# A deformable convolution and eight expert convolutions: groups of x and of the first layer's result kept in SBUF, the last stage in chunks of eight rows, the table's zeros on another queue

## The chip, the cores and the metric

The kernel runs on one core of one Trainium2 chip, in float32. The metric is device time in microseconds, as the median of several runs. Beside those runs there is one profiled execution, which takes longer; all durations of single instructions are from it.

## What is computed

x has shape (2, 256, 128, 128). Two layers follow each other, each with a residual. `_gn` is a group normalisation over groups of eight channels.

```python
def _L0_conv_ref(x, w_conv, b_conv, w_off, b_off, w_mask, b_mask):
    offset = _conv2d(x, w_off, b_off)                   # 3x3, 18 channels
    mask = sigmoid(_conv2d(x, w_mask, b_mask))          # 3x3, 9 channels
    py, px = base_y + dy, base_x + dx                   # 9 sampling points a pixel
    sampled = _deform_sample(x, py, px) * mask          # bilinear, four corners
    return einsum('bckhw,ock->bohw', sampled, w_conv) + b_conv
x = x + _L0_conv_ref(_gn(x), ...)
# eight experts: 256 -> 8 channels by 1x3, 8 -> 256 channels by 3x1, weighted by probs
x = x + _L1_conv_ref(_gn(x), ...)
```

## The kernel before, in words

Rows of an image are handled in groups of eight (GR) and chunks of four (CR). An image has 16 groups; a group of x, 128 partitions by 2 by 1024 numbers, is 1 MB.

**Table.** Bilinear samples are fetched from a table in DRAM, one for each image. A cell of it holds the 256 normalised channels of a pixel and of the pixel below it (`CELL`, 2 KB), so two neighbouring cells, 4 KB, hold all four corners. Around the image lies a frame of zeros, written by six DMAs a table (lines 130 to 138).

**Head** (lines 396 to 468). Image 0 is loaded (16 tiles `xa`), its statistics are taken (line 411), x is normalised in place (`head_norm`, line 431), transposed by TensorE (`hpt`, line 186), copied from PSUM by ScalarE and VectorE in turn (lines 455 and 457) into `hpx`, which has two buffers, and stored to table 0 (line 194). From the third group on, four of the pieces that compute the first group's offsets (`offsets_of`) are put between groups.

**Stream** (lines 735 to 794). One unit is a row of 128 pixels with one of nine taps; there are 2304. A unit takes one gather by GpSimd's queue (line 513, 128 rows of 4 KB, 15 buffers), one product on ScalarE (line 523), three multiply-adds on VectorE (line 529), two transposes (line 539), for each second unit a copy from PSUM (line 547), and one matmul of 128x512 (line 554), which the profile counts as two instructions, as every float32 matmul. Each engine runs its instructions in the order in which this loop emits them: unit s + 15 is gathered, s + 3 multiplied, s added up, s - 8 matmul-ed. Further work is put into slots of the same loop by `put(slot, piece)`: the loads of x (line 492), offsets of a later group (`offsets_of`, lines 279 to 392), the residual (line 563), statistics (line 567) and the store of a finished group to x1 in DRAM (line 570).

Beside image 0's units, `table_beside` (line 573) builds image 1's table: it loads the image twice, once for statistics and once to normalise, transpose and store, each in steps of eight rows. Beside image 1's units, `experts` (line 632) does the second layer for image 0.

**Experts.** A chunk of four rows is loaded from x1 (`xc`, line 640), normalised (line 645), taken through the 1x3 weights into `ph` (line 662), scaled (line 669), taken through the 3x1 weights into two tiles `pe` for even and odd rows (`back`, line 676, and `back_beside`, line 691, for the neighbouring rows), added to xc (line 705) and stored (line 710).

**Tail** (lines 797 to 807). When all units are done, the last statistics are closed and the experts of image 1 run alone, in the order of rows, loads six chunks ahead.

SP's queue carries all plain DMAs but the zeros and issues them in program order: a DMA that waits holds up those behind it.

Of the kernel before, what the change touches and what calls it, by code (L numbers as in the profile page):

```python
# [28 lines left out]
F32 = mybir.dt.float32  # L29
I32 = mybir.dt.int32  # L30
# [35 lines left out]
LM = 8  # L66


@with_exitstack
def layers(ctx, tc, x, w_om, b_om, w_cv, b_cv, w_in, w_out, probs, out):  # L70
    nc = tc.nc

    def view(t, b):
# [31 lines left out]
    base_i = cp.tile([P, GR, NO], I32, name="base_i")  # L105
    nc.gpsimd.memset(base_i, 0)
    nc.gpsimd.iota(
        base_i[:, :, 0:K2].rearrange("p r (i j) -> p r i j", i=3),
        pattern=[[1, GR], [1, 3], [0, 3]], base=-1, channel_multiplier=0,
    )  # L110
    nc.gpsimd.iota(
        base_i[:, :, K2 : 2 * K2].rearrange("p r (i j) -> p r i j", i=3),
        pattern=[[0, GR], [0, 3], [1, 3]], base=-1, channel_multiplier=1,
    )
    base = cp.tile([P, GR, NO], F32, name="base")
    nc.vector.tensor_copy(base, base_i)
    plain = cp.tile([P, GR, NO], F32, name="plain")
# [10 lines left out]


    for t in tables:  # L130
        side = t[WP - 1 : WP - 1 + (HP - 1) * WP].rearrange("(r c) e -> r c e", c=WP)[:, 0:3]
        z3 = zero.unsqueeze(1).broadcast_to([P, 3, CELL])
        nc.scalar.dma_start(t[0:P], zero)
        nc.scalar.dma_start(t[P : WP - 1], zero[0 : WP - 1 - P])
        nc.scalar.dma_start(t[(HP - 1) * WP + 2 : (HP - 1) * WP + 2 + W], zero)
        nc.scalar.dma_start(side[0:P], z3)
        nc.scalar.dma_start(side[P : HP - 1], z3[0 : HP - 1 - P])
        nc.scalar.dma_start(t[HP * WP - 1 : HP * WP + 2], zero[0:3])
# [51 lines left out]
    def store_cells(b, j, px, r, n):  # L190
# [3 lines left out]
        nc.sync.dma_start(cells(b, GR * j - 1 + r, n), pairs)  # L194

    def store_last(b, px):

        nc.sync.dma_start(cells(b, H - 1, 1)[:, 0, 0:C], px[:, GR])
# [3 lines left out]
    def offset_pieces(norm, oc, psum, tag, name):  # L202
# [3 lines left out]
        spread = oc.tile([P, NH, P], F32, name=f"spread_{name}")  # L206
        nb = oc.tile([P, NU], F32, name=f"nb_{name}")
        by_row = oc.tile([P, 3, NO], F32, name=f"by_row_{name}")
# [58 lines left out]

    stream = ExitStack()
    ctx.enter_context(stream)
    up = pool(stream, "u", 1)  # L270
    ip = pool(stream, "idx", 2)
    p_m = pool(stream, "p_m", 3, space=PSUM)
# [6 lines left out]
    def offsets_of(b, g, given=None):  # L279
# [40 lines left out]
        def t(name, shape, dt=F32):  # L320
            held[name] = ip.tile(shape, dt, tag=name, name=f"{name}_{nm}")
# [74 lines left out]
    with ExitStack() as s:  # L396
        hx = s.enter_context(tc.tile_pool(name="hx", bufs=NG))
# [7 lines left out]
        for g in range(NG):  # L405
            xt = hx.tile([P, NH, GN], F32, tag="hx", name=f"xa_{g}")
# [443 lines left out]
```

## Time and profile before

| | |
|---|---|
| median of 3 runs | 3816.98 us (3816.57 to 3818.22) |
| profiled execution | 4171.85 us, span 4169.7 us, mean TensorE clock 0.944 |
| busy | PE 3546.7 us, DVE 3397.1, ACT 1850.5, POOL 2336.0 |
| moved by DMA | 1469.56 MB, 352 GB/s over the span |
| of this, gathers | 1208.11 MB; plain DMAs of SP 255.41 MB; zeros 2.67 MB |
| last statistic of the head ends | 54.6 us |
| first gather issued | 155.8 us |
| last tap of the stream done | 3969.5 us |

PE is TensorE, PEld its weight loads, DVE VectorE, ACT ScalarE, POOL GpSimd, SP the engine that issues DMAs. A group line of the profile names the source line, the engine, the output and inputs, the shapes, the count, busy time and the mean of one. Busy time is no proof of a bound: what matters is what the last wait in a stage is for.

### The profile page before, as it was taken

Reading aid. Unit: us, or ns where it says so; the run is one execution under the profiler, and the core shown is the slowest. Engines: PE = TensorE matmul, PEld = TensorE weight load, DVE = VectorE, ACT = ScalarE, POOL = GpSimd, SP = SyncE. Lnnn points to the kernel's source line nnn. Section 1 sums busy time; section 2 is a strip of 40 time slices with the busy share of each in tenths; the row PEclk is TensorE's granted clock in tenths of the full one; section 3 lists DMA queues with packets and bytes.
Section 4 is the critical chain, followed back from the end, with each engine's and each line's share of the span. In section 5 each row is a group of like instructions: output and inputs, shape, how many; then the busy total and the mean of one; then the engine's idle time right before and its main releaser. Section 6 shows DMA issues by size and latency. Waiting matters only on the chain. (4 is left out here: it accounts for less than half of the span.)

```text
span 4169.7 us, 52967 instructions
## 1 busy us (share of the span) xinstructions
PE 3546.7 (85%) x14684; PEld 1894.1 (45%) x14684; DVE 3397.1 (81%) x7906; ACT 1850.5 (44%) x3899; POOL 2336.0 (56%) x2337
## 2 busy tenths in 40 slices
PE   3588888888878888888888989988988999988999
PEld 2443334444434444443444444444444444444466
DVE  6499998888878888888888888888888888888822
ACT  2244444545445444444444444444444444444432
POOL 0366655666656656666666665665656566655400
PEclk9699999999999999999999999999999999999999
DMA  9999999999999999999899999999999999989754
GB/s 366 391 367 378 389 361 342 377 380 394 354 384 374 404 357 402 386 383 353 326 351 371 350 352 349 359 364 332 357 351 362 347 367 359 364 325 336 293 187 152
DMA packets 434024, 1469.56 MB, mean 352 GB/s; under 512 B 42030, under 2 KB 43182, under 8 KB 433604
## 3 DMA queue, kind: packets, MB, share of 16 engines
q0 software_dynamic: 331776, 1208.11, 76.7%
q1 hardware_dynamic: 100544, 255.41, 16.3%
q8 instruction: 119, 1.95, 0.2%
q10 hardware_dynamic: 1412, 2.67, 0.2%
q14 instruction: 173, 1.42, 0.1%
HBM read 1328.61 MB, written 137.41 MB: 352 GB/s over the span
## 5 line engine op out<-in xcount | busy, mean ns | idle before, releaser
L529 DVE SCALAR_TENSOR_TENSOR acc<-g,wt,acc 128x256 f32<-128x256 f32 x6912 | 3005.3, 481 | 437.6 <-ACT acc L523 289.9
L513 POOL DMA_INDIRECT g<-table,cidx x2304 | 2324.6, 1009 | 1476.1 <-DVE acc L529 489.5
L554 PE MATMUL po<-sm,wcv 128*128 128x512 f32 x4608 | 2481.3, 621 | 300.6 <-DVE x L563 118.0
L547 ACT COPY sm<-ptr 128x512 f32<-128x512 f32 x1152 | 672.5, 584 | 1840.1 <-PE ptr L539 1126.8
L539 PEld LDWEIGHTS ptr<-idp,acc 128*128 128x128 f32 x4608 | 604.3, 145 | 1652.2 <-issue 1017.7
L523 ACT ACTIVATE acc<-g,wt 128x256 f32<-128x256 f32 x2304 | 1064.1, 506 | 104.7 <-DMA g<-table,cidx 75.4
L539 PE MATMUL ptr<-idp,acc 128*128 128x128 f32 x4608 | 939.0, 286 | 177.4 <-ACT sm L547 63.7
L554 PEld LDWEIGHTS po<-sm,wcv 128*128 128x128 f32 x4608 | 747.9, 197 | 368.4 <-ACT sm L547 149.5
L300 PE MATMUL pu<-wus,x 128*128 128x81 f32 (+2 forms) x1600 | 296.7, 313 | 11.6 <-DMA x<-in_x_dram 9.8
L300 PEld LDWEIGHTS pu<-wus,x 128*128 128x128 f32 x1600 | 238.9, 199 | 14.4 <-DMA x<-in_x_dram 10.3
L705 DVE TENSOR_TENSOR xo<-pe,xc 128x512 f32<-128x512 f32 x128 | 85.0, 686 | 187.5 <-PE pe L691 157.2
L662 PE MATMUL ph<-xcn,win 128*64 128x254 f32 (+1 forms) x1536 | 192.9, 399 | 12.1 <-issue 8.1
L662 PEld LDWEIGHTS ph<-xcn,win 128*64 128x64 f32 x1536 | 109.9, 143 | 74.5 <-issue 22.7
L563 DVE SCALAR_TENSOR_TENSOR x<-po,bcv,x 128x512 f32<-128x512 f32 x128 | 95.5, 746 | 54.3 <-remote 27.9
L676 PE MATMUL pe<-h,wout 128*128 128x256 f32 x512 | 132.0, 390 | 0.3 <-issue 0.3
L669 ACT ACTIVATE h<-ph,pr 128x256 f32<-128x256 f32 x64 | 30.5, 476 | 181.2 <-PE ph L662 134.6
L645 ACT ACTIVATE xcn<-xc,shift,rstd 128x512 f32<-128x512 f32 x128 | 100.0, 806 | 1.4 <-DMA xc<-x 1.4
L676 PEld LDWEIGHTS pe<-h,wout 128*128 128x128 f32 x512 | 91.0, 192 | 20.8 <-issue 12.2
L567 DVE BATCH_NORM_STATS2 stats<-x 128x6 f32<-128x512 f32 x128 | 87.6, 684 | 0.1
L691 PE MATMUL pe<-h,wout 64*128 64x128 f32 x1008 | 74.7, 285 | 0.8 <-issue 0.8
L691 PEld LDWEIGHTS pe<-h,wout 64*128 64x128 f32 x1008 | 62.4, 187 | 16.6 <-issue 16.2
L315 PE MATMUL om<-u,idp 128*128 128x216 f32 x192 | 53.8, 362 | 17.6 <-ACT u L309 16.4
(85 smaller groups left out, 638.6 us busy)
## 6 DMA issues: line engine op xcount, KB each, us to landing
g<-table,cidx POOLq DMA_INDIRECT x2304
x<-in_x_dram SPq DMA_DIRECT2D x32, 1024.0 KB
x<-x SPq DMA_DIRECT2D x32, 1024.0 KB
table<-tpx SPq DMA_DIRECT2D x16, 2048.0 KB
xc<-x SPq DMA_DIRECT2D x64, 512.0 KB
out_dram<-xo SPq DMA_DIRECT2D x64, 512.0 KB
table<-hpx SPq DMA_DIRECT2D x15, 2048.0 KB
xa<-in_x_dram SPq DMA_DIRECT2D x16, 1024.0 KB
```

Source lines behind the costliest of these rows:

```text
L300: nc.tensor.matmul(held["ps", j][:, lo:hi], lhsT=xt[:, h, r * W : (r + 1) * W], rhs=w[:, lo - i + 2 : hi - i + 2], start=(i == 2 and h == ...
L513: nc.gpsimd.indirect_dma_start(out=gt[:], out_offset=None, in_=tables[b][:, :], in_offset=bass.IndirectOffsetOnAxis(ap=idx[:, rr, k : k + ...
L523: nc.scalar.activation(acc, gts[u][:, 0:C], AF.Copy, scale=wt[:, 0, rr, k : k + 1])
L529: nc.vector.scalar_tensor_tensor(accs[u], gt[:, q * C : (q + 1) * C], wt[:, q, rr, k : k + 1], accs[u], ALU.mult, ALU.add)
L539: nc.tensor.transpose(pts[u // 2][:, h, (r % 2) * W : (r % 2 + 1) * W], acc[:, h * P : (h + 1) * P], ident)
L547: nc.scalar.copy(sms[u // CR][:, :, (r - 1) * W : (r + 1) * W], pts.pop(u // 2))
L554: nc.tensor.matmul(pos_[b, ci, m], lhsT=wcv[:, h, k, m * P : (m + 1) * P], rhs=sms[u // CR][:, h], start=(k == 0 and h == 0), stop=(k == K ...
L563: nc.vector.scalar_tensor_tensor(v, pos_.pop((b, ci, m)), bcv[:, m : m + 1], v, ALU.add, ALU.add)
L645: nc.scalar.activation(ns[ci][:, h], xs[ci][:, h], AF.Identity, bias=shift[:, h : h + 1], scale=rstd[:, h : h + 1],)
L662: nc.tensor.matmul(o[:, :, to], lhsT=win[:, h, tap], rhs=rows[:, t, :, of], start=(n == 0), stop=(n == 5),)
L676: nc.tensor.matmul(ps[t][:, m], lhsT=wout[:, 2 * t, m * P : (m + 1) * P], rhs=hs[ci], start=(m == 0), stop=False,)
L691: nc.tensor.matmul(ps[t][:, m, j * W : (j + 1) * W], lhsT=wout[half, 1 + 2 * t, m * P : (m + 1) * P], rhs=hs[c][half, i * W : (i + 1) * W] ...
```

## The change

- **x stays.** Two pools outside the stream hold groups of x: `x` and `x_stay`, three buffers each. The head loads groups 0 to 5 of image 0 straight into them and normalises them into two further buffers (`hn`) in place of the tile itself; the stream doesn't load them again. Because there are only two of these, the first group's offset pieces now come between the row pairs of groups 0 and 1, and the third group is normalised after them.
- **The result stays.** The last three groups of image 0 and the last six of image 1 aren't stored to x1. The experts take them from SBUF, and go through the chunks from the last to the first.
- **Experts in place.** The sum is written over xc, and stored from there; the pool of `xo` is gone. Image 0 has four xc buffers and one normalised one (three and two before).
- **Tail by eight rows.** Image 1's experts take chunks of eight rows: matmuls of up to 512 columns, `pe` of two banks each, additions and stores by half of the channels, normalising put earlier.
- **Zeros.** The twelve DMAs of the tables' frames go from ScalarE's queue at the start to SP's queue, behind x and the weights.
- **Room.** `table_beside` works in steps of four rows (64 loads of 512 KB and 32 stores of 1 MB for 32 loads of 1 MB and 16 stores of 2 MB); temporaries of the offsets have one buffer except the cell numbers and weights; some constants live shorter.

The diff, cut to its core:

```diff
@@ -64,6 +64,7 @@
...
 LM = 8
+XB, XR = 3, 3
@@ -126,16 +127,17 @@
...
-    for t in tables:
+    def frame(b):
+        t = tables[b]
...
-        nc.scalar.dma_start(t[0:P], zero)
...
-        nc.scalar.dma_start(side[0:P], z3)
...
+        nc.sync.dma_start(t[0:P], zero)
...
+        nc.sync.dma_start(side[0:P], z3)
@@ -265,10 +267,24 @@
...
+    xp = pool(ctx, "x", XB, side="right")
+    xr = pool(ctx, "x_stay", XR, side="right")
+    def x_tile(b, g):
+        if g >= NG - XR or b == 0 and XB <= g < XB + XR:
+            return xr.tile([P, NH, GN], F32, tag="xr", name=f"x_{b}_{g}")
+        return xp.tile([P, NH, GN], F32, tag="xt", name=f"x_{b}_{g}")
+    def stays(b, g):
+        return g >= NG - XR - (XB if b == B - 1 else 0)
...
+    iq = pool(stream, "idx_1", 1)
@@ -318,7 +334,9 @@
...
-            held[name] = ip.tile(shape, dt, tag=name, name=f"{name}_{nm}")
+            held[name] = (ip if name in ("cidx", "wt") else iq).tile(
+                shape, dt, tag=name, name=f"{name}_{nm}"
+            )
@@ -394,7 +412,8 @@
...
-        hx = s.enter_context(tc.tile_pool(name="hx", bufs=NG))
+        hx = s.enter_context(tc.tile_pool(name="hx", bufs=NG - XB - XR))
+        hn = s.enter_context(tc.tile_pool(name="hn", bufs=2))
         hp = s.enter_context(tc.tile_pool(name="hpx", bufs=2))
@@ -403,7 +422,10 @@
...
-            xt = hx.tile([P, NH, GN], F32, tag="hx", name=f"xa_{g}")
+            if g < XB + XR:
+                xt = xts[0, g] = x_tile(0, g)
+            else:
+                xt = hx.tile([P, NH, GN], F32, tag="hx", name=f"xa_{g}")
             nc.sync.dma_start(xt, xv[:, :, g * GN : (g + 1) * GN])
             xs.append(xt)
@@ -423,19 +445,25 @@
...
+        for b in range(B):
+            frame(b)
...
         def head_norm(g):
+            v = xs[g]
+            if g < XB + XR:
+                xs[g] = hn.tile([P, NH, GN], F32, tag="hn", name=f"xn_{g}")
             nc.scalar.activation(
-                xs[g][:, 0], xs[g][:, 0], AF.Identity, bias=shift[:, 0:1], scale=rstd[:, 0:1]
+                xs[g][:, 0], v[:, 0], AF.Identity, bias=shift[:, 0:1], scale=rstd[:, 0:1]
             )
             nc.vector.tensor_scalar(
-                xs[g][:, 1], xs[g][:, 1], mean[:, 1:2], rstd[:, 1:2], ALU.subtract, ALU.mult
-            )
+                xs[g][:, 1], v[:, 1], mean[:, 1:2], rstd[:, 1:2], ALU.subtract, ALU.mult
+            )
@@ -446,7 +474,7 @@
...
-            if g + 1 < NG:
+            if g != 1 and g + 1 < NG:
                 head_norm(g + 1)
@@ -456,19 +484,20 @@
...
                 if g == 0:
-                    store_cells(0, g, px, i, 2)
+                    store_cells(0, -1, px, i, 2)
+                for piece in samples[: 2 if g < 2 else 1]:
+                    piece()
+                del samples[: 2 if g < 2 else 1]
+            if g == 1:
+                head_norm(2)
             if g > 0:
-                store_cells(0, g, px, 0, GR)
-            if g > 1:
-                for piece in samples[:4]:
-                    piece()
-                del samples[:4]
+                store_cells(0, GR * g - 1, px, 0, GR)
             last = px
-        store_last(0, last)
+        store_last(0, last[:, GR])
@@ -488,9 +517,9 @@
...
     def load_x(b, g):
-        xt = xp.tile([P, NH, GN], F32, tag="xt", name=f"x_{b}_{g}")
-        nc.sync.dma_start(xt, view(x, b)[:, :, g * GN : (g + 1) * GN])
-        xts[b, g] = xt
+        if (b, g) not in xts:
+            xts[b, g] = x_tile(b, g)
+            nc.sync.dma_start(xts[b, g], view(x, b)[:, :, g * GN : (g + 1) * GN])
@@ -571,22 +600,22 @@
...
-        xq = pool(sides, "tx", 2)
+        xq = pool(sides, "tx", 3)
         pq = pool(sides, "tpx", 2)
...
-            held[what, j] = xq.tile([P, NH, GN], F32, tag="tx", name=f"{what}_{b}_{j}")
-            nc.sync.dma_start(held[what, j], xv[:, :, j * GN : (j + 1) * GN])
-        def of_stats(j, i, h):
-            nc.vector.bn_stats(stats[:, h, j * CPG + i], held["xs", j][:, h, i * N : (i + 1) * N])
+            held[what, j] = xq.tile([P, NH, N], F32, tag="tx", name=f"{what}_{b}_{j}")
+            nc.sync.dma_start(held[what, j], xv[:, :, j * N : (j + 1) * N])
+        def of_stats(j, h):
+            nc.vector.bn_stats(stats[:, h, j], held["xs", j][:, h])
@@ -601,11 +630,11 @@
...
-        for j in range(NG):
+        for j in range(NCH):
             put(slot, lambda j=j: load(j, "xs"))
-            for n, (i, h) in enumerate((i, h) for i in range(CPG) for h in range(NH)):
-                put(slot + 16 + 4 * n, lambda j=j, i=i, h=h: of_stats(j, i, h))
-            slot += 16
+            for h in range(NH):
+                put(slot + 14 + 4 * h, lambda j=j, h=h: of_stats(j, h))
+            slot += 8
...
-        for j in range(NG):
+        for j in range(NCH):
             put(slot, lambda j=j: load(j, "xt"))
...
-            for n, i in enumerate(range(0, GR, 2)):
+            for n, i in enumerate(range(0, CR, 2)):
                 put(slot + 26 + 4 * n, lambda j=j, i=i: turn_rows(j, i))
                 put(slot + 28 + 4 * n, lambda j=j, i=i: keep_rows(j, i))
-            put(slot + 42, lambda j=j: store_cells(b, j, held["px", j], 0, GR))
-            slot += 44
-        put(slot, lambda: store_last(b, held["px", NG - 1]))
-        return slot + 1
-    def experts(b, norm, pools, psum, tag, put_, first, step, ahead):
-        cxp, cnp, chp, cop = pools
+            put(slot + 33, lambda j=j: store_cells(b, CR * j - 1, held["px", j], 0, CR))
+            slot += 22
+        put(slot + 14, lambda: store_last(b, held["px", NCH - 1][:, CR]))
...
+    def experts(b, norm, pools, psums, put_, rows, order, first, step, ahead, early=0):
+        cxp, cnp, chp = pools
+        (php, phtag), (pep, petag) = psums
...
+        n, nj = rows * W, rows // 2
+        count = H // rows
+        banks = NH * n // 2 > 512
         def load(ci):
-            xs[ci] = cxp.tile([P, NH, N], F32, tag="cx", name=f"xc_{b}_{ci}")
-            nc.sync.dma_start(xs[ci], x1v[b][:, :, ci * N : (ci + 1) * N])
+            g, r = divmod(ci * rows, GR)
+            if (b, g) in xts:
+                xs[ci] = xts[b, g][:, :, r * W : r * W + n]
+                return
+            xs[ci] = cxp.tile([P, NH, n], F32, tag="cx", name=f"xc_{b}_{ci}")
+            nc.sync.dma_start(xs[ci], x1v[b][:, :, ci * n : (ci + 1) * n])
@@ -649,87 +686,88 @@
...
-            for n, (h, tap) in enumerate(((0, 1), (1, 1), (0, 0), (1, 0), (0, 2), (1, 2))):
+            ps["h"] = php.tile([P, 512], F32, tag=phtag, name=f"ph_{b}_{ci}")
...
         def back(ci, m):
             for t in range(2):
                 if m == 0:
-                    ps[t] = psum.tile([P, NH, N // 2], F32, tag=tag, name=f"pe_{b}_{ci}_{t}")
...
-                    start=(m == 0), stop=False,
+                    start=(banks or m == 0), stop=False,
...
+            own, edge = slice(0, (nj - 1) * W), slice((nj - 1) * W, nj * W)
+            low, rest = slice(0, W), slice(W, nj * W)
+            parts = [(0, ci, rest, own), (1, ci, own, rest), (0, ci - 1, low, edge), (1, ci + 1, edge, low)]
+            parts = [part for part in parts if 0 <= part[1] < count]
...
+                for i, (t, c, to, of) in enumerate(parts):
+                    half = slice(ER, P) if t == 0 else slice(0, ER)
+                    nc.tensor.matmul(
+                        ps[t][:, m, to], lhsT=wout[half, 1 + 2 * t, m * P : (m + 1) * P],
+                        rhs=hs[c][half, of], start=False,
+                        stop=(banks or m == NH - 1) and all(part[0] != t for part in parts[i + 1 :]),
+                    )
+        def total(ci, t, m):
+            ms = slice(0, NH) if m is None else slice(m, m + 1)
+            v = xs[ci][:, ms].rearrange("p h (j t x) -> p t h j x", t=2, x=W)[:, t]
             nc.vector.tensor_tensor(
-                rows(ps["xo"]), ps[t].rearrange("p h (j x) -> p h j x", x=W), rows(xs[ci]), ALU.add
-            )
-        def store(ci):
...
-            del xs[ci]
...
-            e = first + step * ci
...
+        def store(ci, m):
+            ms = slice(0, NH) if m is None else slice(m, m + 1)
+            nc.sync.dma_start(ov[:, ms, ci * n : (ci + 1) * n], xs[ci][:, ms])
+            if m in (None, NH - 1):
+                del xs[ci]
...
-                    put_(e + 2 * h, lambda ci=ci, h=h: normalise(ci, h))
+                    put_(e - early + 2 * h, lambda ci=ci, h=h: normalise(ci, h))
...
+                at_ = e + 20
+                for m in range(NH) if banks else (None,):
+                    for t in range(2):
+                        put_(at_, lambda c=c, t=t, m=m: total(c, t, m))
+                        at_ += 2 if m is None else 0
+                    put_(at_ - (m is None), lambda c=c, m=m: store(c, m))
+                    at_ += 1
@@ -755,8 +793,9 @@
...
-        pools = expert_pools(sides, 3, 2, 4, 2)
-        experts(0, norms1[0], pools, p_m, "m", put, slot + 36, 33, 33)
+        pools = expert_pools(sides, 4, 1, 4)
+        psums = ((p_m, "m"), (p_m, "m"))
+        experts(0, norms1[0], pools, psums, put, CR, range(NCH - 1, -1, -1), slot + 36, 33, 33)
@@ -783,7 +822,7 @@
...
-                if m == NH - 1 and ci % CPG == CPG - 1:
+                if m == NH - 1 and ci % CPG == CPG - 1 and not stays(b, ci // CPG):
                     put(s + 4, lambda b=b, g=ci // CPG: store_x1(b, g))
@@ -798,10 +837,13 @@
...
-    p_m = pool(ctx, "p_e", 8, space=PSUM)
-    pools = expert_pools(ctx, 8, 3, 4, 4)
+    psums = (pool(ctx, "p_h", 2, space=PSUM), "h"), (pool(ctx, "p_e", 3, space=PSUM), "e")
+    pools = expert_pools(ctx, 10, 3, 4)
     tail = defaultdict(list)
-    experts(1, norms1[1], pools, p_m, "e", lambda slot, piece: tail[slot].append(piece), 0, 24, 24 * 6)
+    experts(
+        B - 1, norms1[B - 1], pools, psums, lambda slot, piece: tail[slot].append(piece), GR,
+        range(NG - 1, -1, -1), 0, 24, 24 * 6, 17,
+    )
```

## The prediction

> **What bounds the kernel now.** I read the page's busy row and its 40 slices first, then the busy time by stage, then the DMA rows of three stretches, then the timeline where the stream ends.
>
> Busy time by stage (start and end in us; busy us of PE, PEld, DVE, ACT, POOL with instruction counts; PE clock, DMA share, GB/s). The rows are: head, first gathers, image 0, image 1, tail.
>
> ```profile
> 0.00:155.00 155.00, 60.23 (x336) 55.13 (x336) 82.68 (x149) 39.45 (x54) 11.35 (x33) 0.87 0.99 368
> 155.00:220.00 65.00, 41.58 (x137) 24.82 (x138) 37.94 (x87) 21.92 (x47) 40.47 (x42) 0.74 0.99 388
> 220.00:2060.00 1840.00, 1553.77 (x5670) 784.14 (x5669) 1599.33 (x3774) 863.91 (x1831) 1135.91 (x1125) 0.94 0.97 375
> 2060.00:3935.00 1875.00, 1670.62 (x6896) 884.10 (x6895) 1604.07 (x3761) 851.53 (x1847) 1141.74 (x1132) 0.96 0.94 351
> ...
> 3964.00:4170.00 206.00, 192.21 (x1545) 132.83 (x1543) 47.64 (x78) 60.56 (x98) 0.00 (x0) 0.98 0.53 172
> ```
>
> The head is DMA (0.99). The stream of 2304 gathers has DMA at 0.94 to 0.97 and VectorE at 86 to 87%, with no other engine nearer. The tail has DMA at 0.53 and TensorE at 93%. So bytes count before 3964 us, and matmul time after it.
>
> DMA rows of 5 to 50 us (x loads, 4 KB packets), then of 80 to 140 us (table stores, 2 KB packets):
>
> ```profile
> DMA packets 5485, 18.37 MB, mean 408 GB/s; under 512 B 350, under 2 KB 350, under 8 KB 5484
> DMA packets 11272, 22.75 MB, mean 379 GB/s; under 512 B 176, under 2 KB 176, under 8 KB 11269
> ```
>
> Both stretches are saturated, so 408 is what 4 KB packets get and 379 what 2 KB packets get. Between 170 and 200 us, gathers alone got 409.
>
> VectorE's longest wait in the list of waits (us in total, times, longest):
>
> ```profile
> DVE acc L529 <- ACT acc L523: 289.9, 78, 10.9
> ```
>
> The timeline at the end of the stream and in the tail (start us, us, instruction, count, idle before):
>
> ```profile
> 3963.20 6.28 PE L554 MATMUL po<-sm,wcv 128*128 128x512 f32 x14
> 3976.66 1.52 ACT L645 ACTIVATE xcn<-xc,shift,rstd 128x512 f32<-128x512 f32 x2 [1.44 <-DMA xc<-x]
> 3989.32 2.80 PE L662 MATMUL ph<-xcn,win 128*64 128x256 f32 x24
> 3992.05 1.99 PE L676 MATMUL pe<-h,wout 128*128 128x256 f32 x8
> 3993.98 1.16 PE L691 MATMUL pe<-h,wout 64*128 64x128 f32 x16
> 3995.07 2.80 PE L662 MATMUL ph<-xcn,win 128*64 128x256 f32 x24
> ```
>
> ACT's product waits for its gather in turn. The last lines give the tail's beat: 3995.07 - 3989.32 = 5.75 us for four rows, TensorE without a gap.
>
> **Which time the sum is made against.** The profiled execution took 4171.85 us (span 4169.7), the median is 3816.98. Its steps are priced in the trace, then carried over. If head (155.8 us to the first gather) and tail (206) last as long untraced, the untraced stream has 3817 - 155.8 - 206 - 2 = 3453 us. It moves 1469.6 MB less 57 (head) less 35 (tail) = 1377 MB, so 399 GB/s, and VectorE's 3267 us of stream work fill 94.6% of it. Here the Trainium skill stands against the row. "Perfetto Trace Analysis", section Roofline, gives some 435 GB/s as the practical ceiling for one core alone; this trace never holds more than about 410. By the row the untraced stream runs at 97% of its DMA and each byte removed is time; by the rule at 92%, below VectorE's share, and little is. I take 0.7 of a byte's price for the stream, 1 and 0 as the ends.
>
> **Part by part.**
>
> *Bytes removed.* A group of x is 1.049 MB. Six x loads of image 0 go (6.3 MB), as do three x1 stores and three x1 loads of image 0 (6.3) and six x1 stores of image 1 (6.3), all in the stream; six x1 loads go in the tail (6.3), where DMA has room. The first three of the x loads lie where the stream starts, at DMA 0.99 with VectorE at 58%: 3.1 MB / 0.408 = 7.7 us, whole. The other 15.7 MB: 38.5 us of DMA time.
>
> *Image 1's table in steps of four rows.* Its 32 loads of 1 MB become 64 of 512 KB, with 2 KB packets: 33.5 MB at 379 in place of 408 is 88.4 - 82.1 = +6.3 us of DMA. Its 16 stores of 2 MB become 32 of 1 MB, packets as before. The skill's "DMA: Bandwidth & Descriptors", section Bandwidth, says to batch to 1 MiB or more, and its Anatomy section puts some 2 us of fixed cost on each DMA: by that, 48 more transfers would cost 96 us. The row says they needn't: the saturated table stores above hold 379 GB/s as several transfers overlap, and the gathers fill the gaps. I take +6.3; the ends are 0 (smaller bursts ahead of gathers could even return a few us) and the 96 of the rival below. ScalarE's normalise becomes 64 x 0.806 (L645, same width) for 32 x 1.236: +12 us on an engine 46% busy. VectorE gets 16 more row copies of 0.298: +4.8, hidden by its idle 13% in the trace; uncovered it would be 4.8 whole.
>
> So the stream beyond its start: 38.5 - 6.3 = 32 us of DMA time, x 0.7 = 22.5.
>
> *Head.* Zeros move from ACT's queue (2.67 MB beside x) to SP's queue behind x and weights. The x loads should then end near 2.5 + 16.8/0.408 = 44 us in place of 52, the last statistic near 47 for 54.5, the first table row 8 us sooner. But the bytes ahead of the table are the same, so only idle DMA can be won: from 50 to 70 us it ran at 0.94 and 0.68, 3.8 us idle. Against it: on SP the 12 zero requests stand before the table stores, with the other requests behind them; and the offset matmuls of the first group (48 at 0.175 = 8.4 us) move from spread over groups 2 to 9 into groups 0 and 1, and group 2's normalise (1.25 us) waits for them, since the unnormalised x stays and only two normalised copies exist. With TensorE at 2.6 us a group plus these, group 1's store comes some 1.3 us after group 0's has drained (5.4 us each). 3.8 - 1.3: -2.5. Ends: -6 (no lag) and +2 (lag doubled, a bubble at group 2).
>
> *Tail.* Per eight rows TensorE needs 2 x 5.75 = 11.5 now: 24 L662 at 0.114, 8 L676 at 0.240 and 16 L691 at 0.068 per four rows. L554's fourteen 512-wide ones run at 0.43 each, so 256 columns cost 0.215, and the fixed part is 0.006 (L662, two halves at once), 0.025 (L676), 0.014 (L691). With the width doubled: 24 x 0.221 = 5.31; 8 x 0.455 = 3.64; L691 becomes 8 of 384 columns at 0.175 and 8 of 128 at 0.068, 1.94. Together 10.9. The run from 3977.5 to 4164.7 is 187.2 us; 16 x 10.9 + 1.4 (start, where ScalarE's wider second half is late) = 175.8: -11.4. The start no longer waits for xc (1.05 us), but its first normalise is 0.44 longer: -0.6. At the end four additions of 0.645 follow the last matmul instead of two: +1.3; the 512 KB store is as long as before. Sum -11, ends -14 (L676 at 0.43 flat, 3.44) and -5 (widths scale with no gain).
>
> *At nothing:* one normalised buffer instead of two for image 0's experts (the next normalise comes 27 slots, over 40 us, after its reader; without that cover ScalarE would wait some 3 us a chunk); single offset temporaries (reused a group later, over 100 us); additions in place; reversed chunks. The four-deep xc buffer is stored 43 slots before it is loaded again, so SP shouldn't block at it.
>
> **Sum.** In the trace at full price: -2.5 - 7.7 - 32 - 11 = -53, a span near 4117. Untraced: -2.5 - 7.7 - 22.5 - 11 = -44, so 3773.
>
> **Rivals.**
> *The whole DMA price.* For it: DMA 0.94 to 0.97, 97% of the best rate seen. Against: in image 1 only 351 GB/s. -53: 3764, to 3745 if the smaller bursts spare gathers some of their 5 to 10 us delays. Chance 0.28.
> *VectorE is the bound untraced.* For it: 94.6%, and 59 additions in 25.81 us at the drained end of the stream, which is 1.31 us a gather. Against: its 290 us of waits for products. Then 22.5 goes and 4.8 is added: -2.5 - 7.7 - 11 + 4.8 = -16, 3801. Chance 0.24.
> *Slower: the halved transfers choke SP's queue.* SP issues in order; a load or a table store that waits for its buffer holds up x, x1 and table rows behind it, and gathers wait for their offsets. For it: SP's queue already waited 283.5 us in 9 times for VectorE's first table row (image 0). Against: per row of image there is as much buffer as before. At 2 us for each of 48 transfers: +96 - 44 = +52, 3869. It decides from 0.9 us each (44 / 48). Chance 0.05.
> My forecast has 0.39, and 0.04 is left for no measurable change.
>
> Faster by over 0.2% (7.6 us, about what measurement can tell from none): 0.39 + 0.28 + 0.24 = 0.91; same 0.04; slower 0.05. The range runs from the first rival's low end, 3745, to just past the VectorE case, 3803.
>
> **What would show it.** Moved bytes near 1444 MB; last statistic near 47 us and first gather near 152; DMA of the stream still over 0.93; tail from the last gathered tap to the end near 195 us in place of 206, beat 10.9 us for eight rows. Wrong: VectorE's share of the stream above 90% in the trace with a span cut under 30 us (then it binds), new SP waits for the table tile, or a head that ends later.

## The result, and the profile after

| | before | after |
|---|---|---|
| median | 3816.82 us (3816.46 to 3818.22, 6 runs) | 3802.51 us (3800.80 to 3803.56, 6 runs) |
| ratio, 95% interval | | 0.9962 [0.9949, 0.9974] |
| profiled execution | 3818.56 us, span 3816.4 (the second) | 3802.63 us, span 3800.9 |

The change saves 14.3 us where 44 were forecast. One thing must be said first, as the numbers can't be understood without it: the profile that the prediction was made from, 4171.85 us, is of a slower execution, not of one that profiling had lengthened. The kernel before, profiled once more, took 3818.56 us, 1 us over the median of the runs beside it. A profiled execution doesn't have to take longer than a run, as the section on the metric says it does. From here on "before" is that second profile, unless the first is named.

Busy time by stage, columns as ahead of the prediction (start and end in us; busy us of PE, PEld, DVE, ACT, POOL; clock, DMA share, GB/s). The kernel before, in its second profile; the rows are head, first gathers, image 0, image 1, tail:

```profile
0.00:155.00 155.00, 58.49 (x336) 53.29 (x336) 82.60 (x149) 39.42 (x54) 11.30 (x33) 0.87 0.99 368
155.00:220.00 65.00, 48.36 (x176) 28.44 (x177) 48.59 (x112) 27.66 (x56) 46.18 (x46) 0.77 1.03 409
220.00:1954.00 1734.00, 1527.03 (x5728) 772.45 (x5729) 1618.57 (x3811) 910.08 (x1854) 1160.96 (x1139) 0.98 1.02 402
1954.00:3609.00 1655.00, 1592.18 (x6900) 856.56 (x6899) 1595.40 (x3757) 866.58 (x1839) 1125.90 (x1120) 1.00 1.01 395
3609.00:3816.00 207.00, 194.12 (x1547) 133.80 (x1546) 48.34 (x79) 61.35 (x98) 0.00 (x0) 0.98 0.53 171
```

The changed kernel, the same stages:

```profile
0.00:155.00 155.00, 65.04 (x348) 58.23 (x348) 82.31 (x149) 39.52 (x54) 10.78 (x33) 0.85 0.99 368
155.00:220.00 65.00, 50.92 (x186) 28.30 (x186) 55.74 (x128) 30.76 (x63) 49.54 (x50) 0.82 1.02 398
220.00:1947.00 1727.00, 1508.95 (x5707) 767.54 (x5706) 1614.54 (x3810) 913.52 (x1878) 1159.94 (x1136) 0.98 1.02 399
1947.00:3602.00 1655.00, 1592.21 (x6897) 856.57 (x6897) 1596.03 (x3759) 863.67 (x1839) 1128.19 (x1120) 1.00 1.00 389
3602.00:3800.00 198.00, 184.00 (x786) 74.25 (x782) 46.84 (x79) 48.88 (x51) 0.00 (x0) 0.97 0.37 141
```

Read image 1's rows first. They last 1655 us in both, although DMA moved 395 GB/s in one and 389 in the other: bytes went and no time did. VectorE is busy 96% of both, not the 86% of the first profile. Where each microsecond went, by the times at which stages end:

| ends at (us) | before | after | difference so far |
|---|---|---|---|
| first gather issued | 155.7 | 155.2 | -0.5 |
| first matmul of a gathered tap | 182.4 | 174.9 | -7.5 |
| statistics of image 1's table closed (starts) | 626.1 | 618.3 | -7.8 |
| statistics of image 0's result closed (starts) | 1953.7 | 1947.4 | -6.3 |
| last 14 matmuls of taps start | 3609.0 | 3602.5 | -6.5 |
| end of the span | 3816.4 | 3800.9 | -15.5 |

So the start of the stream gave 7 us, the tail 9, and the 3400 us between them gave back 1.

**What the first profile showed and was not read.** ScalarE's two large groups in the first profile of before (count, busy us, mean ns, then idle us before them and what ended it):

```profile
L523 ACT ACTIVATE acc<-g,wt 128x256 f32<-128x256 f32 x2304 | 1064.1, 506 | 104.7 <-DMA g<-table,cidx 75.4 <-DVE acc L529 19.1 <-issue 6.9
L547 ACT COPY sm<-ptr 128x512 f32<-128x512 f32 x1152 | 672.5, 584 | 1840.1 <-PE ptr L539 1126.8 <-remote 441.8 <-issue 200.5
```

The same two in its second profile:

```profile
L523 ACT ACTIVATE acc<-g,wt 128x256 f32<-128x256 f32 x2304 | 1105.2, 506 | 640.1 <-DMA g<-table,cidx 522.7 <-DVE acc L529 102.2 <-DVE stats L567 2.2
L547 ACT COPY sm<-ptr 128x512 f32<-128x512 f32 x1152 | 666.5, 579 | 964.8 <-PE ptr L539 963.5
```

In the first, the product waited 75.4 us in all for gathers; the rest of ScalarE's idleness lies before its copy, 642 us of it put down to "remote" or "issue", which is to nothing that the profile names. In the second there is none of that, and gathers are waited for seven times as long. One such stop, in the timeline of the first profile (start, us, instruction, idle before):

```profile
699.95 0.38 PE L539 MATMUL ptr<-idp,acc 128*128 128x128 f32 x2
...
703.70 0.95 POOL L513 DMA_INDIRECT g<-table,cidx  x1 [0.30 <-issue]
707.10 0.59 ACT L547 COPY sm<-ptr 128x512 f32<-128x512 f32 x1 [11.40 <-remote]
...
708.46 1.00 DVE L529 SCALAR_TENSOR_TENSOR acc<-g,wt,acc 128x256 f32<-128x256 f32 x2 [8.69 <-ACT acc L523]
```

ScalarE stood from 695.7 until 707.1, and for the last 6.8 us of that every transpose ahead of its copy was done (700.3). VectorE ran out of products and stood 8.7 us; after 703.7 no gather was issued until ScalarE went on. From the first gather to 3600 us, gaps of 3.5 us and more before ScalarE's instructions come to 770 us in 126 places in the first profile and to 57 us in 10 in the second. The executions lie 353 us apart, and this is the large difference between their profiles. That it is why VectorE and DMA both looked short of full is read from these rows; no run switched the stops off.

### The profile page after: what moved, and what is told of

The parts are those of the page before. It is cut to its first block, busy times and chain, and to the rows that moved or that the text cites. A ratio compares the mean times of both kernels' runs of the same rounds, so it can differ in the third digit from the quotient of the medians.

```text
span 3800.9 us, 51362 instructions
## 1 busy us (share of the span) xinstructions
PE 3401.1 (89%) x13916; PEld 1784.9 (47%) x13916; DVE 3395.5 (89%) x7922; ACT 1896.3 (50%) x3883; POOL 2348.4 (62%) x2337
## 2 busy tenths in 40 slices
DMA packets 427186, 1444.29 MB, mean 380 GB/s; under 512 B 42110, under 2 KB 43262, under 8 KB 426772
## 5 line engine op out<-in xcount | busy, mean ns | idle before, releaser
L583 PE MATMUL po<-sm,wcv 128*128 128x512 f32 x4608 | 2398.4, 602 | 180.8 <-DVE x L592 100.5
L552 ACT ACTIVATE acc<-g,wt 128x256 f32<-128x256 f32 x2304 | 1103.7, 506 | 624.3 <-DMA g<-table,cidx 538.7
L568 PE MATMUL ptr<-idp,acc 128*128 128x128 f32 x4608 | 913.9, 280 | 114.2 <-DVE acc L558 65.5
L699 PE MATMUL ph<-xcn,win 128*64 128x254 f32 (+3 forms) x1152 | 177.3, 457 | 3.1 <-ACT xcn L682 3.1
L737 DVE TENSOR_TENSOR xc<-pe,xc 128x512 f32<-128x512 f32 x92 | 60.4, 684 | 97.1 <-issue 79.1
L713 PE MATMUL pe<-h,wout 128*128 128x256 f32 (+1 forms) x384 | 125.6, 456 | 1.1 <-DVE xc L737 1.1
L699 PEld LDWEIGHTS ph<-xcn,win 128*64 128x64 f32 x1152 | 78.9, 138 | 80.8 <-issue 51.1
L706 ACT ACTIVATE h<-ph,pr 128x256 f32<-128x256 f32 (+1 forms) x48 | 26.3, 547 | 142.8 <-PE ph L699 142.8
L728 PE MATMUL pe<-h,wout 64*128 64x128 f32 (+1 forms) x752 | 69.3, 321 | 0.0
L682 ACT ACTIVATE xcn<-xc,shift,rstd 128x512 f32<-128x512 f32 (+1 forms) x72 | 65.8, 926 | 0.0
## 6 DMA issues: line engine op xcount, KB each, us to landing
xt<-in_x_dram SPq DMA_DIRECT2D x32, 512.0 KB, 13.5
```

The source lines that it names most:

```text
L552: nc.scalar.activation(acc, gts[u][:, 0:C], AF.Copy, scale=wt[:, 0, rr, k : k + 1])
L568: nc.tensor.transpose(pts[u // 2][:, h, (r % 2) * W : (r % 2 + 1) * W], acc[:, h * P : (h + 1) * P], ident)
L583: nc.tensor.matmul(pos_[b, ci, m], lhsT=wcv[:, h, k, m * P : (m + 1) * P], rhs=sms[u // CR][:, h], start=(k == 0 and h == 0), stop=(k == K ...
L699: nc.tensor.matmul(o[:, :, to], lhsT=win[:, h, tap], rhs=pairs[:, t, :, of], start=(q == 0), stop=(q == 5),)
L713: nc.tensor.matmul(ps[t][:, m], lhsT=wout[:, 2 * t, m * P : (m + 1) * P], rhs=hs[ci], start=(banks or m == 0), stop=False,)
L737: nc.vector.tensor_tensor(v, ps[t][:, ms].rearrange("p h (j x) -> p h j x", x=W), v, ALU.add)
```

## Theories

**V:** in an execution of 3817 us VectorE sets the pace of nearly the whole stream (how far that goes is seen after experiment 5). Bytes removed from it leave 15 gathers in the queue as before, DMA's share stays near 1, and the time stays. Gains are left where VectorE has room (the start of the stream) and where the stream is over (tail).

**B:** DMA sets the pace, as forecast, and the removed bytes' 38.5 us were earned but lost again to something the change added: the four-row table steps, the zeros on SP's queue, waits for kept tiles.

## Experiments

The first four ran on one chip, beside 26 runs of the kernel before (3817.47 us).

**1. The kernel before, profiled again.** No edit.

> The kernel before, unchanged, for a second profiled execution. Theory V (VectorE binds the stream in an ordinary execution, and the first trace was of an execution slower than the timed ones): span near 3815 us, VectorE above 94% of the stream of image 1, last tap near 3608 us, first gather near 155.8, tail 206. Theory B (the trace is typical, bytes are the bound, and the change's gain was lost elsewhere, in the table steps of four rows): span near 4170 again, VectorE near 86%.

Measured: 3818.56 us; the profile was used above.

**2. The tail alone undone.** Chunks of four rows, in the new order, in place:

```diff
-    ... (pool(ctx, "p_e", 3, space=PSUM), "e")
+    ... (pool(ctx, "p_e", 6, space=PSUM), "e")
-        B - 1, ..., GR, range(NG - 1, -1, -1), 0, 24, 24 * 6, 17,
+        B - 1, ..., CR, range(NCH - 1, -1, -1), 0, 24, 24 * 6,
```

> The changed kernel with the tail in chunks of four rows, in place and from SBUF as now. Both theories: the tail's beat goes from 10.84 us for eight rows to 2 x 5.75 = 11.5, so +8 to +10 us from 3802.5, to about 3811. If the tail's start or end makes up for it, +4.

Measured: 3810.30 us (15 runs), 0.9981 [0.9973, 0.9989] of the kernel before. The eight-row chunks, with the `pe` tiles and the earlier normalising that go with them, are worth 7.8 us of the tail's 9.0.

**3. Nothing of the result stays.** All groups are stored to x1 and loaded again:

```diff
     def stays(b, g):
-        return g >= NG - XR - (XB if b == B - 1 else 0)
+        return False
```

> The changed kernel with every group of the first layer's result stored to x1 and loaded again (18.9 MB more: 9.4 stored, 9.4 loaded, 6.3 of the loads in the tail). Theory V: image 1 waits for VectorE at 97.5%, so +1 to +6 us, of which 1 to 5 at the tail's start, where the first chunk must be loaded. Theory B: 12.6 MB in the stream at 0.4 MB/us are 31 us, so +30 to +36.

Measured: 3805.82 us, 0.9968 [0.9956, 0.9981]; moved 1463.18 MB for 1444.29. Of the 18.9 MB more, 12.6 belong to the stream by the prediction's count (the last of the stores, 1 MB, is requested just behind it, at 3609.9 us), where 31 us is the price of DMA (12.6 / 0.408), and 6.3 to the tail. All of it costs 3.3 us (3.7 between the two profiles). In the profiles the last 14 matmuls of taps start at 3602.8 us for 3602.5, and image 1's taps last 1655.2 us again; the other 3.4 us lie in the tail, where the first chunk must now be loaded (ScalarE's first normalise waits 4.2 us for it). B falls here: if bytes had been earned and lost elsewhere, giving them back would have cost their price.

**4. The kept groups of x loaded again.** The six loads come back, into the same tiles:

```diff
             xts[b, g] = x_tile(b, g)
-            nc.sync.dma_start(xts[b, g], view(x, b)[:, :, g * GN : (g + 1) * GN])
+        nc.sync.dma_start(xts[b, g], view(x, b)[:, :, g * GN : (g + 1) * GN])
```

> The changed kernel, but the stream loads groups 0 to 5 of image 0 again into the tiles where they already lie (6.3 MB more). Theory V: VectorE is at 97.7% from 200 to 700 us, where most of these loads fall, so 0 to +5 us, the most at the stream's start. Theory B: 6.3 / 0.4 = +15 us.

Measured: 3808.81 us, 0.9978 [0.9969, 0.9987], 6.3 us over the changed kernel. That is more than V expected, but the place is V's: the first tap's matmul comes at 181.4 for 174.9, and from there nothing is added. The first three loads cost 6.5 us where VectorE has room, the other three nothing. Experiments 3 and 4 together put back all 15.7 MB that the prediction priced beyond the stream's start.

**5. Less for VectorE.** The statistics of image 1's first-layer result are left out, and its second normalisation uses made-up ones; 64 instructions of 0.684 us, 44 us of VectorE, go beside image 1's units:

```diff
     def result_stats(b, ci, m):
+        if b == 1:
+            return
...
+    nc.vector.memset(stats1[1], 1.0)
```

On a chip where the kernel before takes 3817.88 us:

> The changed kernel without 64 statistics of VectorE (44 us) in image 1. Where the kernel before takes 3817 us and ScalarE doesn't stand still: theory V, image 1 at 662 MB / 0.408 = 1622 us for 1655, so 3772, 30 us under the changed kernel; theory D (DMA binds): within 5 us of 3802. Where it takes 4230 us: 0.991 of it, as three times before.

Measured: 3773.37 us (3772.73 to 3775.84), 0.9883 [0.9867, 0.9900] of the kernel before, 29.1 us under the changed kernel's 3802.51 (measured beside a kernel before of 3816.82). This is the run that V stood or fell with. Image 1 in the changed kernel, then in this one (columns as before):

```profile
1947.40:3602.50 1655.10, 1592.31 (x6901) 856.92 (x6899) 1595.96 (x3759) 863.84 (x1840) 1127.79 (x1120) 1.00 1.00 389
```

```profile
1947.30:3575.70 1628.40, 1581.17 (x6900) 862.81 (x6899) 1561.73 (x3697) 883.58 (x1840) 1130.43 (x1120) 1.00 1.01 396
```

And ScalarE's product in that stretch, in the changed kernel, then here:

```profile
L552 ACT ACTIVATE acc<-g,wt 128x256 f32<-128x256 f32 x1128 | 521.6, 504 | 31.1 <-DMA g<-table,cidx 28.4 <-DVE acc L558 1.9
```

```profile
L552 ACT ACTIVATE acc<-g,wt 128x256 f32<-128x256 f32 x1128 | 539.9, 506 | 248.4 <-DMA g<-table,cidx 213.7 <-DVE acc L558 28.1 <-DVE pm L345 1.3
```

Not a byte fewer was moved, and 26.7 us of the stretch went. V had expected it to stop at 1622 us, where DMA would bind; it took 1628.4. The DMA share, 1.00 and 1.01, can't tell the two apart; the wait for gathers can: 28 us while VectorE is the bound, 214 us once it has given way.

Why 44 us of work brought less than 44 has two parts. The 44 us is a sum of durations, and instructions that follow each other overlap a little: VectorE's busy time in the two rows falls by 34.2 us (1595.96 to 1561.73). Of these, 26.7 shorten the stretch, and the rest is new idle time. Probably gathers set the pace before all of it was gained; TensorE, busy for 97% of the shorter stretch, may have a part in it, which no run separates.

**Where V doesn't hold.** The same wait, read stage by stage in the kernel before, sorts the stream. Where it starts (155 to 220 us) ScalarE's product waits 44 of 65 us for gathers, and there bytes paid. From 220 to 620 us it waits 47 of 400, with VectorE busy for 97.7%, and there they didn't. While image 1's table is written (640 to 1780 us) it waits 359 of 1140:

```profile
L523 ACT ACTIVATE acc<-g,wt 128x256 f32<-128x256 f32 x741 | 372.8, 508 | 452.7 <-DMA g<-table,cidx 359.3 <-DVE acc L529 83.2 <-DVE stats L567 2.0
```

VectorE is busy for 91% of that third of the stream, so V is too wide: gathers set its pace at least in part. The change took only one store of 1 MB out of it (requested at 1731.8 us in the kernel before). What a byte is worth there, no run here shows.

**The same and other edits on chips where ScalarE stands still.** These runs fell on four other chips, on which the kernel before takes 4168 to 4233 us. The expectations come first, then one table. Three edits are new: the kernel before without those statistics (the edit of 5); the kernel before with image 1's table in steps of four rows and nothing else; and the changed kernel with image 1's statistics on ScalarE and the zeros requested behind the third group's table store:

```diff
     def load(j, what):
-            held[what, j] = xq.tile([P, NH, GN], ...)
+            held[what, j] = xq.tile([P, NH, N], ...)
...
-        for j in range(NG):
+        for j in range(NCH):
```

```diff
+    def sum_up(sums, h, j, v):
+        nc.scalar.activation(junk, v, AF.Copy, accum_out=sums[:, 0, h, j : j + 1])
+        nc.scalar.activation(junk, v, AF.Square, accum_out=sums[:, 1, h, j : j + 1])
...
-        for b in range(B):
-            frame(b)
...
+            if g == 2:
+                for b in range(B):
+                    frame(b)
```

The changed kernel itself:

> The changed kernel itself, unchanged, beside the kernel before. Where the kernel before takes 4232 us (as on the chip of the last runs, and about as in the first profile of the kernel before, which took 4171.85): if bytes are the price there, as the prediction reckoned from that profile, -44 to -53 us; if VectorE with the waits between gather, product and addition sets the pace there too, -16 us (head, stream start, tail) plus the -9 to -13 of the four-row steps, so -25 to -30. Where it takes 3817 us: 3802 again.

The changed kernel without the statistics, three times:

> The changed kernel without the statistics of image 1's first-layer result: 64 instructions of VectorE of 0.684 us (44 us) are left out beside image 1's units, and the second layer's normalisation of image 1 uses made-up statistics. Theory V (VectorE binds the stream at 97%, the removed bytes lie under it): image 1's 1655 us shrink until DMA binds, at 662 MB / 0.408 = 1622, so about -30 us against the changed kernel. Theory D (DMA binds, and the removed bytes were lost to something else): within 5 us of the changed kernel.

> The changed kernel without the 64 statistics of VectorE (44 us) beside image 1's units, with made-up statistics; once more, since the chip of the runs before this had the kernel before at 4231 us. Where the kernel before takes 3817 us, theory V (VectorE binds image 1 at 97%): image 1's 1655 us shrink until DMA binds, at 662 MB / 0.408 = 1622, so about -30 us against the changed kernel, 3772. Theory D (DMA binds): within 5 us of 3802. Where it takes 4231 us again: -39 us against the kernel before, as measured there.

> The changed kernel without 64 statistics of VectorE (44 us) in image 1, now beside the changed kernel on one chip. Where the kernel before takes 3817 us, theory V: -30 us against the changed kernel (image 1 at 662 MB / 0.408 = 1622 for 1655), theory D: within 5 us. Where it takes 4232 us: -12 to -28 us against the changed kernel, by how much VectorE counts there.

The kernel before without them, three times:

> The same left out of the kernel before: 44 us of VectorE beside image 1's units, with made-up statistics. Theory V: image 1 still moves 671 MB here, so DMA stops it at 671 / 0.408 = 1645, about -10 to -15 us against the kernel before; the difference to the same edit in the changed kernel, 15 to 20 us, is what image 1's removed bytes are worth once VectorE has given way. If VectorE's time alone counts, both gain the same 30 to 44 us; theory D: both within 5 us of their base.

> The same left out of the kernel before. Where that takes 3817 us, theory V: image 1 moves 671 MB, so DMA stops it at 671 / 0.408 = 1645, 10 to 15 us against the kernel before; what the changed kernel gains more, 15 to 20 us, is what its fewer bytes are worth once VectorE has given way. If VectorE's time alone counts: the same 30 to 44 us in both. Theory D: within 5 us of 3817.

> The kernel before without 64 statistics of VectorE (44 us) in image 1, with made-up statistics. Where the kernel before takes 3818 us: theory V with bytes: image 1 moves 671 MB here for 662 in the changed kernel, so it stops at 1645, 10 to 15 us under the kernel before, and the changed kernel's 29 us less show what its removed bytes are worth once VectorE has given way. If VectorE's time alone counts there: 29 us here too. Where it takes 4170 to 4230 us: 0.993 to 0.996 of it, as twice before.

Table steps of four rows, twice:

> The kernel before with image 1's table built in steps of four rows and nothing else of the change. Theory V: the wider stretch where VectorE binds does not see it, but the stretch in which image 1's table is written, where DMA binds, does: +1.5 us as the two traces differ there, up to +5 with the 16 more row copies of VectorE. Theory of packet size (2 KB packets at 379 GB/s instead of 408): +6.3. Theory of 2 us fixed for each of 48 more DMAs: +96.

> The kernel before with image 1's table in steps of four rows and nothing else. Where the kernel before takes 3817 us: +1.5 to +5 us by theory V (only the stretch that writes the table is bound by DMA, and VectorE has 16 more row copies), +6.3 by the packet rates that the prediction used, +96 by 2 us for each of 48 more DMAs; if four-row transfers spare the gathers, -5 to -13, as on the slower chip.

Statistics on ScalarE, four times:

> The changed kernel with image 1's statistics, of the table's input and of the first layer's result, taken by ScalarE (a sum and a sum of squares, two passes of 0.81 us) instead of VectorE (0.684 us), 128 times, and with the zeros requested behind the third group's table store. Theory V: 44 us less of VectorE in the first statistics stretch and 44 us less in image 1, each until DMA binds: -15 to -20 in the first, -25 to -30 in image 1, -2 in the head, so -40 to -50 us. Theory D: -2 us, or slower if ScalarE's 200 us more delay the products.

> The changed kernel with image 1's statistics taken by ScalarE in two passes (128 times) instead of VectorE, and the zeros requested behind the third group's table store. Where the kernel before takes 3817 us, theory V: -15 to -20 in the first statistics stretch, -25 to -30 in image 1, -2 in the head: -40 to -50 us against the changed kernel, 3755 to 3762. Theory D: within 5 us of 3802, or slower if ScalarE's 200 us more delay the products.

> The changed kernel with image 1's statistics by ScalarE (128 times two passes) in place of VectorE, and the zeros requested behind the third group's table store. Where the kernel before takes 3818 us, theory V, which the run without statistics in image 1 bore out with 29 us: the same 29 us again in image 1, 15 to 20 in the first statistics stretch before DMA binds, 2 in the head: 3752 to 3760. If ScalarE's two passes delay its products: less, by up to all of it. Where it takes 4230 us: as before on such chips, within 5 us of the changed kernel.

> The changed kernel with image 1's statistics by ScalarE in place of VectorE, and the zeros requested behind the third group's table store. Where the kernel before takes 3818 us, theory V: 3752 to 3760, a good 1.1% under the changed kernel. If ScalarE's two passes delay its products, less. Where it takes 4170 to 4230 us: 0.992 to 0.999 of the kernel before, as three times there.

| kernel | medians (us) | of the kernel before, run beside it |
|---|---|---|
| changed | 4213.05 | 0.9968 [0.9956, 0.9980] |
| changed, no statistics | 4192.31, 4196.24, 4182.11 | 0.9913, 0.9915, 0.9909 (about +-0.0024) |
| before, no statistics | 4208.78, 4205.02, 4202.32 | 0.9955, 0.9933, 0.9955 (+-0.0024 or less each) |
| before, table by four rows | 4218.07, 4223.95 | 0.9978 [0.9964, 0.9991], 0.9970 [0.9958, 0.9983] |
| changed, statistics on ScalarE | 4220.51, 4229.11, 4132.68, 4216.75 | 0.9982, 0.9991, 0.9920, 0.9975 (+-0.0020 or less each) |

ScalarE's copy in the changed kernel on such a chip (idle us, times):

```profile
  PE ptr L568: 1143.6, 643
  remote: 518.3, 88
```

So these chips show the picture of the first profile, and these rows say what would have followed from it. *The change* is worth 0.32% there (10.6 us by the medians, 13.5 by the ratio), no more than on the other chips: even with VectorE at 84% of image 1 (1603.9 of 1908 us) the bytes are not paid in time. Here too the product hardly waits for gathers (41 us in the whole stream), so the first profile didn't show a price of bytes even for executions of its own kind. It is less than the 25 to 30 us expected, too; since single profiles on these chips differ by 10 us and more in a stage, where the rest went stays open. *VectorE's work* is: the 44 us bring 19 to 28 us in the kernel before, and 25 (by the ratios) to 31 us (by the medians) in the changed one. The changed kernel doesn't gain clearly more from losing them than the kernel before (0.32% and 0.52% on average make 0.84%, 0.88% were measured), so the latent 15 to 20 us that V promised for the bytes didn't appear here. *Four-row table steps*, for which 6.3 us were booked as a cost, bring 9 to 13 us there, and cost nothing near the 96 that the prediction worked out from the Trainium skill's 2 us a DMA. Alone on a chip with 3817 us they weren't tried.

*Statistics on ScalarE* failed as an improvement. In three of four runs the kernel lies above the ratio of the changed kernel; one, on the chip with 4168 us, is better (0.9920), beside no run of the changed kernel. The engine that takes the work is the one that stands still: the first statistics, closed at 651.1 us in the changed kernel on one of these chips, are closed at 680.8, 684.7, 660.9 and 686.4 in the four profiles of this. None of its runs was on a chip with 3817 us, so whether it wins there is open.

Its other half is informative. With the zeros moved behind the third group, the first table store starts at 56.0 to 56.4 us in place of 61, as hoped, and still the first gather comes at 162.5 to 164.4, 6 to 9 us later than the changed kernel's 155.2 (156.2 on a chip of this kind). DMA, in the changed kernel (50 to 70 us; its shares are 0.72 and 0.94 on a chip of this kind), then in this one (the second of its four profiles):

```profile
50.00:60.00 10.00, 6.95 (x34) 6.45 (x35) 3.44 (x11) 3.53 (x5) 0.00 (x0) 1.00 0.74 232
60.00:70.00 10.00, 9.71 (x74) 8.83 (x72) 4.01 (x6) 4.99 (x9) 0.80 (x2) 1.00 1.01 371
```

```profile
50.00:60.00 10.00, 6.83 (x36) 6.33 (x37) 3.57 (x11) 3.71 (x5) 0.00 (x0) 1.00 0.46 129
60.00:70.00 10.00, 9.71 (x75) 8.87 (x74) 4.26 (x7) 5.16 (x9) 1.18 (x2) 1.00 0.60 221
```

At the start of the table TensorE, which computes the first offsets there as well, is busy for 9.7 of 10 us while DMA stands at 0.60: rows come more slowly than DMA stores them. The zeros filled that hole; moved out of it, they cost about their bytes in full (estimated at 2.67 MB / 0.379 = 7.0 us).

## Why the prediction failed, point by point

- **The 0.7 of a byte's price, in "Which time the sum is made against", is the step that failed.** It made 22.5 us of the 15.7 MB removed beyond the stream's start, and none of them came. On the chips with 3817 us, 12.6 MB put back into the stream cost 0.3 us (experiment 3) and the loads beyond its start nothing (experiment 4); on the chips with the first profile's picture the change is worth 10.6 to 13.5 us, not 44. The sum held averages of the whole stream against each other, VectorE's 94.6% against 97% of DMA. VectorE's average was right: it is 94.5% in the second profile. But the stages differ, 97.7% from 220 to 620 us, 91% from 640 to 1780, 96% in image 1, and but for one store of 1 MB the 15.7 MB lay from 220 to 620 us, from 1780 to 1950 (97.5%), in image 1 or, the last store, just behind it.
- **The missing 29.7 us.** 22.5 are this term; head and tail are short by 2.0 each, the stream's start by 0.7, the table's stretch lost 1.5, and about 1 is the difference between profiles and medians.
- **The reading that carried it** was that "ACT's product waits for its gather in turn". ScalarE's own row said 75.4 us; VectorE's longest waits were for a ScalarE that stood still. DMA at 0.94 to 0.97 with a VectorE that stalls looked like a bound by DMA, and wasn't one where the bytes were removed.
- **The rival "VectorE is the bound untraced"**, at 3801 and 0.24, is what came nearest (3802.5), and only for its sake did the range reach that far. The sign named for it, "VectorE's share of the stream above 90% in the trace with a span cut under 30 us", is met: 93% in image 0, 96% in image 1, and 15.5 us. Of its terms, the 4.8 us of row copies is smaller: the stretch that writes the table (from 626.1 to 1953.7, and from 618.3 to 1947.4) grew by 1.5 us. That its sum is met within 1 us is partly luck: head, start and tail fell short by 4.7 us, and the 4.8 by 3.3. Nor is VectorE the bound in the table's stretch.
- **The roofline rule** (the Trainium skill, "Perfetto Trace Analysis", section Roofline) would have put DMA at 92% by its ceiling of 435 GB/s, below VectorE. The stages of the stream move 395 to 409 GB/s in the second profile, at DMA shares of 1.01 to 1.03 and never 435, so the row's ceiling stands. That little was to be had from bytes came out all the same, but not because DMA had room: where the bytes were, VectorE is at 96 to 98%.
- **Stream start, -7.7:** right, -7.0 between the first gather and the first tap's matmul; and experiment 4 puts 6.5 of it down to these loads.
- **Tail, -11:** -9.0. The beat was right: TensorE without a gap, 10.84 us for eight rows (forecast 10.9).

```profile
3766.09 5.34 PE L699 MATMUL ph<-xcn,win 128*64 128x512 f32 x24
3776.93 5.34 PE L699 MATMUL ph<-xcn,win 128*64 128x512 f32 x24
...
3789.96 2.81 PE L713 MATMUL pe<-h,wout 128*128 128x512 f32 x6 [1.06 <-DVE xc L737]
```

  Two ends were short-changed. The last chunk waits 1.06 us for an addition, as only three `pe` tiles exist; and the first two passes into `ph` take 13.9 us for 10.6, of which 1.06 is a wait for ScalarE and the rest goes with a granted clock of 0.82 (3616 to 3630 us), after 7 us in which TensorE had little to do. The prediction put 1.4 us on this start, though its own trace has it too: two passes worth 5.6 us took 8.8 there (3977.5 to 3986.3).
- **Head, -2.5:** -0.5, within its range. The last statistic ended at 48 us (47 forecast), but the saved time wasn't there to be had: SP was busy with the zeros until 61.

```profile
53.89 0.52 SPq L135 DMA_DIRECT2D table<-zero  x1
...
60.22 0.73 SPq L140 DMA_DIRECT2D table<-zero  x1
61.05 2.96 SPq L196 DMA_DIRECT2D table<-hpx  x3
```

  From this view alone the queue looks guilty. The run with the zeros behind the third group says otherwise: earlier stores without the zeros left DMA idle, and the first gather came later. DMA's idle time from 50 to 70 us only fell from 3.7 us (shares 0.94 and 0.69) to 2.6 (0.74 and 1.01).
- **Four-row steps, +6.3 of DMA:** not seen. The table's stretch lasts 1327.6 us in the kernel before and 1327.6 to 1329.1 in the five profiles with four-row steps on these chips, and most of it is the stretch where gathers are waited for, so a cost in DMA time should show. Alone the steps gave back 9 to 13 us where ScalarE stands still. Neither the 379 GB/s of 2 KB packets fits, nor the fixed cost from the Anatomy section of the Trainium skill's "DMA: Bandwidth & Descriptors", which is given there for DMAs that GpSimd issues, while SP issues these.

## What to carry to other kernels

Compare a profiled execution with the timed runs before using it: if it is 9% longer, ask which engine stands idle for nothing that the profile names, and profile again, since such a trace shows other bounds than the runs have. A DMA share near 1 isn't a bound where many transfers are kept queued; look, stage by stage, at how long the consumer waits for them (28 us of 1655 in image 1, 359 of 1140 beside the table), and price a byte only where that wait is long. Work taken off a full engine pays at once (26.7 us for 34.2 of busy time), bytes under it don't.

## What was not expected of the hardware

- ScalarE can stand still 3.5 to 13 us at a time, over a hundred times in an execution, part of it with its input ready. It was so on four of the six chips that the experiments ran on, for the same program, and goes with 350 to 415 us more. What stops it is not shown; the profile puts much of it down to "remote" or "issue". TensorE's granted clock is lower in these executions too (0.93 to 0.95 for about 0.98); which follows from which, no run here tells.
- On these chips image 1's table in half steps was the better one (0.2 to 0.3%), though its loads shrink from 1 MB to 512 KB and their packets from 4 to 2 KB. Whether that comes from the transfers is open: the same edit gives the loads three buffers for two, halves ScalarE's normalising instructions and moves slots.
